# Residual and second norm of two batches moved into the next attention stage, with y turned to tokens ahead by VectorE, in a kernel of attention and triangle attention

## The chip, the cores and the metric

The kernel runs on one core of a Trainium2 chip. The time is device microseconds of one execution. Before the change it is 3651.67, the median of 3 runs (3650.98 to 3653.79). The engines are named as in the profile: PE is TensorE (PEld its weight loads), DVE is VectorE, ACT is ScalarE, POOL is GpSimd, SP is the engine whose queue issues most DMAs.

## The reference

Four images x of 64x64 pixels and 256 channels go through two layers. Layer 0 is self-attention over the 4096 pixels; layer 1 is triangle attention on the 64x64 grid with 8 heads, followed by an MLP. Only these lines of layer 1 matter for the change (x_in is the output of layer 0, called y in the kernel):

```
attn_out = out.reshape(B, N, N, E) @ Wo
h = x_in + attn_out
h = _layer_norm(h, ln_agg_g, ln_agg_b)
mlp = relu(h @ W1 + b1) @ W2 + b2
h = mlp + h
return _layer_norm(h, ln_out_g, ln_out_b)
```

A norm takes mean and variance over the 256 channels of a pixel (a token), so it is easy where tokens lie in the partitions and channels along the free side. Layer 0 leaves y the other way round, with channels in the partitions.

## The kernel before, in words

The batches are worked one after the other. Each batch has an attention stage (layer0) and then a triangle stage. The tokens of a batch, that is the code quoted above, run one stage later: next_layer1 for batch b, with b from 1 to 3, carries the tokens of batch b - 1. Batch 3's tokens have no later stage; two of their 16 tiles start in the triangle stage of batch 3, and the rest run in alone, the closing stage.

**Attention stage.** There are 8 query blocks of 512 pixels, each with 8 steps; a step is counted by g from 0 to 63, and k = g mod 8 is its place in its block. In a step TensorE makes four score tiles for the next step (L544) and multiplies four tiles of exponentials e with the values (L571); ScalarE takes the exponentials (L556); VectorE adds e into esum (L578), which frees one of e's two buffers. After each step comes a part of the block before it, from the list parts: k = 0 sums esum over partitions on TensorE (L596), takes the reciprocal on VectorE (L600), scales the output (L602) and reduces the denominators to bounds (L610); k = 1 projects the output to y (L623, L624 adds bias and input); k = 2 to 7 project y to q, k and the two values (L638, L670). In layer 0 of batch 0 VectorE also turns the other batches' inputs with 32x32 block transposes (L348), eight each second step. In the attention stages of batches 2 and 3, every third step brings one tile of finished tokens back from memory (recall) and GpSimd applies the last gain and shift (finish, L1248 and L1249). VectorE works its queue in the order of the program: values(g), the parts, and then whatever is added at the end of the step.

**Passage.** After step 63 the last block's output, its projections, the first loads of the triangle stage (fetch_v2, fetch_qk) and the first token tile are interleaved by hand, on queues of SP and ScalarE.

**Triangle stage.** There are 32 steps of 8 products (L999), made of attention weights and values, of 128x2048 elements each. In an even step 3 of the 8 products go to GpSimd and 5 to VectorE, in an odd step 2 and 6; TensorE adds each product up (L1009). Two steps and one token tile make a period. The order of a period is written by hand in ORDER: a word is an action, and /1 or /2 says how many periods late it runs. R05 is product 5 of the even step, A05 its accumulation, R1x and A1x those of the odd step; T takes an accumulator to SBUF; t turns weights on TensorE, c copies GpSimd's share of them to SBUF, S and W make the softmax sums and weights; sp and e are the scores of a later pair of heads and their exponentials. They end four tiles ahead of the stage's end. The triangle stage of batch 0 has an order of its own and no tokens. VectorE has three product buffers, GpSimd two. The words for tokens are:

- h0, h1: heads, TensorE: the attention output times Wo (L1081), and onto it y, turned to tokens by TensorE with the identity (L1086)
- sa: statistics of the sum, VectorE (L1097, L1098); rr: rsqrt for both norms as ln and exp, ScalarE (L1124, L1126); pp: a Newton step for both norms, seven small operations on GpSimd (L1142 to L1153)
- fa: the first norm applied, ScalarE (L1158); ht: h turned to channels, TensorE (L1181); hT and hU: two copies of it with gain and shift, ScalarE (L1186), one for the MLP and one as residual
- m, r, z: the MLP, TensorE and ScalarE (L1214, L1223, L1234); z also turns the residual copy back and adds it in PSUM (L1240)
- so: sums of the result for the second norm, ScalarE (L1112, L1116); fo: that norm applied, ScalarE (L1158); fi: the result stored (put_off) for recall in the next attention stage, or, for batch 3's stage, finished at once

**Closing stage.** alone works one tile of batch 3's tokens per round: heads, statistics on VectorE, MLP, with the residual and the second norm on VectorE (L1205, L1206, L1106).

## Time and profile before

| | us |
|---|---|
| median of 3 runs | 3651.67 |
| the profiled execution: its time | 3654.27 |
| its span | 3652.5 |
| a period of the triangle stage of batch 1, steady | 27.76 |
| a round of the closing stage | 9.51 |
| a transpose at L1086, mean | 0.273 |
| a product on VectorE (L999), mean | 2.274 |
| a product on GpSimd (L999), mean | 4.576 |

The profile is of one execution. A group's mean is the length of one instruction, and neighbouring instructions of one engine overlap in these records; what an engine has to pay for an instruction is the distance from its start to the next one's start, when nothing waits. Busy time of a stretch is the union of the records in it. "Idle before" is what the engine waited ahead of the instruction and for whom. In the stretches, x with a number is a count of instructions.

### The profile page before, as it was taken

Reading aid. Unit: us, or ns where it says so; the run is one execution under the profiler, and the core shown is the slowest. Engines: PE = TensorE matmul, PEld = TensorE weight load, DVE = VectorE, ACT = ScalarE, POOL = GpSimd, SP = SyncE. Lnnn points to the kernel's source line nnn. Section 1 sums busy time; section 2 is a strip of 40 time slices with the busy share of each in tenths; the row PEclk is TensorE's granted clock in tenths of the full one; section 3 lists DMA queues with packets and bytes.
Section 4 is the critical chain, followed back from the end, with each engine's and each line's share of the span. In section 5 each row is a group of like instructions: output and inputs, shape, how many; then the busy total and the mean of one; then the engine's idle time right before and its main releaser. Section 6 shows DMA issues by size and latency. Waiting matters only on the chain.

```text
span 3652.5 us, 58549 instructions
## 1 busy us (share of the span) xinstructions
PE 3544.0 (97%) x22410; PEld 1909.6 (52%) x22410; DVE 2739.5 (75%) x2326; ACT 1934.8 (53%) x4209; POOL 1805.7 (49%) x918
## 2 busy tenths in 40 slices
PE   9999899988999999999999999999999999999998
PEld 6555444434555555554455555554455555555477
DVE  4777599996555479999565549999755556999976
ACT  3444455544444367666444457676544436777654
POOL 5000199994000068889311028889722106999910
PEclk9999999999999999999999999999999999999999
DMA  9544555465111343425422153333522225341221
GB/s 174 140 130 121 137 150 143 118 135 126 52 49 52 97 116 95 94 51 104 101 80 79 58 144 92 78 89 66 129 73 78 75 83 137 91 96 47 68 69 52
DMA packets 487987, 353.38 MB, mean 97 GB/s; under 512 B 302673, under 2 KB 433489, under 8 KB 478865
## 3 DMA queue, kind: packets, MB, share of 16 engines
q1 hardware_dynamic: 438656, 322.58, 33.1%
q0 software_dynamic: 36160, 19.94, 5.1%
q10 hardware_dynamic: 12880, 7.01, 0.7%
q8 instruction: 179, 2.93, 0.3%
q14 instruction: 112, 0.91, 0.1%
HBM read 197.34 MB, written 152.04 MB: 96 GB/s over the span
## 4 chain that ended last, share of the span: by engine, by line
PE 68%; POOL 5%; DVE 4%; issue 3%; ACT 2%; DMA 1%; SPq 0%; ACTq 0%; DVEq 0%; POOLq 0%
PE o L571 18%; PE acc L1009 15%; PE proj L638 6%; PE mp L1214 6%; PE zp L1234 5%; PE s L544 5%; POOL Rp L999 4%; DVE R L999 3%; PE sp L897 3%; PE hp L1081 3%; PE v1p L670 2%; PE y L623 1%; PE att L951 1%; PE htp L1181 1%; PE hp L1086 1%
## 5 line engine op out<-in xcount | busy, mean ns | idle before, releaser
L999 POOL TENSOR_TENSOR Rp<-attP,v 128x2048 f32<-128x2048 f32 x328 | 1491.1, 4576 | 463.3 <-ACT attP L959 367.8
L999 DVE TENSOR_TENSOR R<-att,v 128x2048 f32<-128x2048 f32 x696 | 1547.7, 2274 | 67.7 <-PE acc L1009 49.4
L571 PE MATMUL o<-e,v 128*128 128x512 f32 x2048 | 1043.6, 592 | 0.0
L578 DVE TENSOR_TENSOR esum<-esum,e 128x2048 f32<-128x2048 f32 x224 | 525.0, 2344 | 508.9 <-ACT e L556 505.6
L556 ACT ACTIVATE e<-s 128x1024 f32<-128x1024 f32 x512 | 523.4, 1024 | 581.3 <-PE s L544 484.6
L544 PE MATMUL s<-gT,fT 128*128 128x512 f32 x1024 | 785.6, 769 | 8.6 <-ACT e L556 5.1
L1009 PE MATMUL acc<-R,wsel 128*32 128x512 f32 x5568 | 705.7, 602 | 37.2 <-DVE R L999 29.4
L571 PEld LDWEIGHTS o<-e,v 128*128 128x128 f32 x2048 | 388.7, 190 | 275.9 <-issue 233.6
L1009 PE MATMUL acc<-Rp,wsel 128*32 128x512 f32 x2624 | 344.3, 596 | 11.1 <-POOL Rp L999 10.4
L1019 ACT COPY ao<-acc 128x1024 f32<-128x1024 f32 x256 | 254.4, 1021 | 189.6 <-PE acc L1009 153.1
L1009 PEld LDWEIGHTS acc<-R,wsel 128*32 128x32 f32 x5568 | 152.1, 109 | 384.5 <-issue 277.9
L544 PEld LDWEIGHTS s<-gT,fT 128*128 128x128 f32 x1024 | 194.2, 190 | 243.9 <-issue 231.0
L1142 POOL TENSOR_SCALAR nt<-mv 128x4 f32<-128x4 f32 (+1 forms) x51 | 9.8, 192 | 627.2 <-DVE mv L1098 623.1
L1248 POOL TENSOR_TENSOR z<-z,log_bc 128x512 f32<-128x512 f32 x48 | 71.8, 1496 | 452.2 <-DMA z<-raw 434.5
L934 ACT ACTIVATE es<-S,rd 128x64 f32<-128x64 f32 x1024 | 257.8, 336 | 16.6 <-DVE rd L926 13.8
L1214 PE MATMUL mp<-hT,w 128*128 128x256 f32 x1024 | 249.5, 389 | 0.7 <-ACT hT L1186 0.7
L1234 PE MATMUL zp<-w,hid 128*128 128x256 f32 x1024 | 245.0, 385 | 0.8 <-ACT hid L1223 0.8
L1214 PEld LDWEIGHTS mp<-hT,w 128*128 128x128 f32 x1024 | 186.8, 190 | 101.2 <-ACT attP L959 36.0
L1234 PEld LDWEIGHTS zp<-w,hid 128*128 128x128 f32 x1024 | 185.7, 190 | 62.3 <-issue 29.3
L600 DVE RECIPROCAL rec<-den 128x512 f32<-128x512 f32 x32 | 107.4, 3358 | 119.4 <-PE den L596 114.0
L1009 PEld LDWEIGHTS acc<-Rp,wsel 128*32 128x32 f32 x2624 | 81.5, 110 | 197.8 <-issue 139.0
L1223 ACT ACTIVATE hid<-mp,b_sb 128x256 f32<-128x256 f32 x256 | 105.2, 469 | 117.7 <-PE mp L1214 117.7
(180 smaller groups left out, 3665.7 us busy)
## 6 DMA issues: line engine op xcount, KB each, us to landing
v<-v2d SPq DMA_DIRECT2D x44, 512.0 KB
v1c<-v1d SPq DMA_DIRECT2D x128, 128.0 KB
aT<-ao SPq DMA_DIRECT2D x1024, 16.0 KB
A<-aT SPq DMA_DIRECT2D x256, 64.0 KB
out_dram<-z SPq DMA_DIRECT2D x63, 256.0 KB
y<-yT SPq DMA_DIRECT2D x56, 256.0 KB
q<-st SPq DMA_DIRECT2D x56, 256.0 KB
k<-st SPq DMA_DIRECT2D x52, 256.0 KB
```

The source lines that it names most:

```text
L544: nc.tensor.matmul(s_ps[r // 2][:, r % 2, :], fT[tt][:, ts(r * 4 + n, P)], gT[qb // 4][:, ts(qb % 4, QB)], start=True, stop=not safe,)
L556: nc.scalar.activation(e[g][:, 2 * j : 2 * j + 2, :], s_ps[j], AF.Exp)
L571: nc.tensor.matmul(o_ps[qb], F.v[tt][:, r * 4 + n, :], es[:, r, :], start=(k == 0 and r == 0), stop=(k == 7 and r == 3),)
L578: nc.vector.tensor_tensor(esum[qb], esum[qb], es, ALU.add)
L638: nc.tensor.matmul(ps, w[:, cc, rows], y(qb, cc), start=(cc == 0), stop=(cc == 1))
L897: nc.tensor.matmul(sp[ts(h, 64), lh, n, :], k[rows, u * 8 + n, :], q[rows, u * 8 + n, :], start=True, stop=True,)
L934: nc.scalar.mul(e[:, i, :], rows[:, i, :], rec[:, i : i + 1])
L999: eng.tensor_tensor(R, src.unsqueeze(1).to_broadcast([P, D, N]), v2[h], ALU.mult)
L1009: nc.tensor.matmul(acc[32 * c : 32 * c + 32, n % 2, :], w[:, n, c, 16 * h : 16 * h + 32], R[:, ts(c, 8), :].rearrange("p d j -> p (d j)"), ...
L1019: nc.scalar.copy(self.ao[step][:, ts(np, 2)].rearrange("p k d j -> p k (d j)"), self.acc[step][np])
L1214: nc.tensor.matmul(self.mp[:, fc % 2, :], w1_sb[:, cc, ts(fc, P)], self.hT[tt][:, cc, :], start=(cc == 0), stop=(cc == 1),)
L1234: nc.tensor.matmul(zp[:, n, :], self.hid[tt][:, fc, ts(n, P)], w2_sb[:, fc, :], start=(fc == 0), stop=(fc == 3 and tt not in self.hT2),)
```

## The change

For the tokens of batches 0 and 1, the residual and the whole second norm leave the triangle stage. There the normed h (carried_off) and the MLP's result (summed_off) are stored separately, and in the attention stage of batches 2 and 3 a chain of six actions per tile, spread over eight steps, does the rest: recall (load of both), settle (VectorE: gain and shift of h, add, statistics), rooted (ScalarE), polished (VectorE), scaled (ScalarE) and finish (GpSimd as before). The statistics of the first norm, in these two stages, go from VectorE to ScalarE.

For batches 0, 1 and 3, y is turned to tokens when it is made: after the fourth step of a block VectorE turns it in square blocks of 32 (turn_y), and four DMAs write it to memory as tokens, for the last block in the passage. TensorE no longer turns it in heads; VectorE adds it to the heads in PSUM (add_y). For batch 2, whose tokens run in batch 3's triangle stage, nothing of this changes.

The triangle stages of batches 1 and 2 get a new order; batch 3's keeps the old one under the name ORDER_LAST. The softmax bounds are kept for one batch at a time and reduced at the start of the next attention stage. The tile that holds y for a token tile has two buffers where it had one.

```diff
 ORDER = """
+    sa R11/2 A13/2 A10/2 A11/2 T01/2 R12/2 sp/1 r0/1 e0/1 e1/1 t0/1 m1/1 R14/2 A12/2 A17/2 fo A14/2 R00/1 V0/1
+    R16/2 T10/2 r1/1 A16/2 c0/1 S1/1 W1/1 rr/1 R07/1 R15/2 A00/1 A15/2 z1/1 R01/1 T11/2 z0/1 pp/1 t1/1 R03/1
+    A01/1 R02/1 so/1 fa A07/1 A03/1 c1/1 R06/1 A02/1 ht hT S0 hU T00/1 fi/1 R05/1 h1/-1 V1/1 h0/-1 m0 R04/1
+    R13/1 W0 sf/1 R10/1 A04/1 A06/1 A05/1 f0/1 R17/1 f1/1
+""".split()
+
+
+ORDER_LAST = """
...
-    dens = ctile([P, NB, 256 + 16], "dens")
+    dens = ctile([P, 256 + 16], "dens")
+    lims = ctile([P, 2, NB], "lims")
+    def limits(b):
+        for j, op in enumerate((ALU.min, ALU.max)):
+            nc.vector.tensor_reduce(lims[:, j, b : b + 1], dens, AX.X, op)
...
-            for cc, tag in enumerate(("A", "yc")):
-                t = work.tile([P, 512], F32, tag=tag, name="yb", bufs=1)
+            for cc, tag, bufs in ((0, "A", 1), (1, "yc", 2)):
...
+        def turn_y(qb, **where):
+            t = work.tile([P, 16, 2, 32], F32, name="yr", **where)
+            for cc in range(2):
+                rows = y(qb, cc).rearrange("p (k t) -> p k t", t=32)
+                for k in range(4):
+                    nc.vector.transpose(t[:, ts(k, 4), cc, :], rows[:, ts(k, 4), :])
+            for r in range(4):
+                nc.sync.dma_start(
+                    out=io["yt"][ts(qb, QB), ts(r, 64)].rearrange("(k t) c -> t k c", t=32),
+                    in_=t[ts(r, 32)].rearrange("t k h c -> t k (h c)"),
+                )
 
...
+        if turned_ahead(b):
+            parts[3].append(lambda qb: turn_y(qb, tag="hid", bufs=1))
...
-            if b > 1 and g % 3 == 0 and g < 3 * NP:
-                rest.recall(NP * (b - 2) + g // 3)
-            if b > 1 and g % 3 == 2 and g < 3 * NP:
-                rest.finish(NP * (b - 2) + g // 3)
+            if b > 1:
+                for do, late in ((rest.finish, 7), (rest.scaled, 6), (rest.polished, 5), (rest.rooted, 4), (rest.settle, 3), (rest.recall, 0)):
+                    if (g - late) % 3 == 0 and 0 <= g - late < 3 * NP:
+                        do(NP * (b - 2) + (g - late) // 3)
+            if g == 1 and b > 0 and not safe:
+                limits(b - 1)
...
         bounds(last)
+        if turned_ahead(b):
+            turn_y(last, tag="k8")
...
-            rest.carried(t0)
+            (rest.carried if b == NB - 1 else rest.carried_off)(t0)
...
+    def turned_ahead(b):
+        return b != NB - 2
...
-        def put_off(self, tt):
+            self.raw, self.both, self.settled = {}, {}, {}
+
+
+        def put_off(self, tt, part, src):
             b, t = divmod(tt, NP)
-            if t == 0:
-                self.raw[b] = dram.tile([NP, P, 2, C], F32, tag="raw", name="raw")
-            nc.sync.dma_start(out=self.raw[b][t], in_=self.z.pop(tt))
+            if b not in self.raw:
+                self.raw[b] = dram.tile([NP, P, 2, 2, C], F32, tag="raw", name="raw")
+            nc.sync.dma_start(out=self.raw[b][t][:, part], in_=src)
+
+        def carried_off(self, tt):
+            self.put_off(tt, 0, self.h.pop(tt))
+
+        def summed_off(self, tt):
+            self.put_off(tt, 1, self.z.pop(tt))
         def recall(self, tt):
             b, t = divmod(tt, NP)
-            self.z[tt] = work.tile([P, 2, C], F32, tag="s4", name="z")
-            nc.sync.dma_start(out=self.z[tt], in_=self.raw[b][t])
+            self.both[tt] = work.tile([P, 2, 2, C], F32, tag="R", name="hz", bufs=3)
+            nc.sync.dma_start(out=self.both[tt], in_=self.raw[b][t])
+
+        def settle(self, tt):
+            both = self.both.pop(tt)
+            h, z = both[:, 0], both[:, 1]
+            nc.vector.tensor_tensor(h, h, lag_bc.unsqueeze(1).to_broadcast([P, 2, C]), ALU.mult)
+            nc.vector.tensor_tensor(h, h, lb2_bc.unsqueeze(1).to_broadcast([P, 2, C]), ALU.add)
+            nc.vector.tensor_tensor(z, z, h, ALU.add)
+            self.z[tt] = z
+            self.stats(z, 2)
+            self.settled[tt] = self.mv
+            self.mv = None
+
+        def rooted(self, tt):
+            self.mv = self.settled.pop(tt)
+            self.roots(2, 4)
+            self.settled[tt], self.mv = (self.mv, self.rs), None
+
+        def polished(self, tt):
+            self.mv, self.rs = self.settled.pop(tt)
+            self.polish(2, 4, nc.vector)
+            self.settled[tt] = self.rn
+
+        def scaled(self, tt):
+            self.rn = self.settled.pop(tt)
+            self.affine(self.z[tt], self.z[tt], 2)
...
-            nc.sync.dma_start(out=yc, in_=io["y"][:, ts(t, 256)].rearrange("(c p) t -> p c t", p=P))
-            self.A[tt] = A, yc
+            src = io["yt"][ts(t, 256)] if turned_ahead(b) else io["y"][:, ts(t, 256)]
+            nc.sync.dma_start(out=yt, in_=src.rearrange("(n p) c -> p n c", p=P))
+            self.A[tt], self.yt[tt] = A, yt
...
             for cc in range(2):
                 nc.tensor.matmul(
                     hp[:, n, :], A[:, cc, ts(n, 2), :].rearrange("p i j -> p (i j)"), wo1_sb[:, cc, :],
-                    start=(cc == 0), stop=False,
-                )
-            for cc in range(2):
-                nc.tensor.matmul(
-                    hp[:, n, ts(cc, P)], yc[:, cc, ts(n, P)], ident, start=False, stop=(cc == 1),
-                    is_transpose=True,
-                )
+                    start=(cc == 0), stop=(cc == 1 and turned_ahead(tt // NP)),
+                )
+            if not turned_ahead(tt // NP):
+                for cc in range(2):
+                    nc.tensor.matmul(
+                        hp[:, n, ts(cc, P)], self.yt[tt][:, cc, ts(n, P)], ident, start=False, stop=(cc == 1),
+                        is_transpose=True,
+                    )
+
+        def add_y(self, tt):
+            hp, yt = self.hps[tt], self.yt.pop(tt)
+            if not turned_ahead(tt // NP):
+                return
+            for n in range(2):
+                own = hp[:, n, :].rearrange("p (h r c) -> p h r c", h=2, r=4)
+                nc.vector.tensor_tensor(own, own, yt[:, n, :].rearrange("p (r h c) -> p h r c", h=2, r=4), ALU.add)
...
         def stats_a(self, tt):
+            self.add_y(tt)
...
             elif word == "sa" and first:
                 moments(q - 1)
-                rest.stats(rest.hps[t0 + q], 0)
+                rest.add_y(tt)
+                if own:
+                    rest.stats(rest.hps[tt], 0)
+                else:
+                    junk = work.tile([P, 2, C], F32, tag="sx", name="junk", bufs=1)
+                    rest.sums_of(rest.hps[tt], junk, rest.mv, 0)
             elif word == "so" and second:
+                z = rest.z[tt] = work.tile([P, 2, C], F32, tag="s4", name="z")
+                if own:
+                    moments(q)
+                    rest.sums_of(rest.zp[tt], z, rest.mv, 2)
+                else:
+                    nc.scalar.copy(z, rest.zp.pop(tt))
+            elif word == "rr" and second and (own or q + 1 < n1):
                 moments(q)
-                z = rest.z[t0 + q] = work.tile([P, 2, C], F32, tag="s4", name="z")
-                rest.sums_of(rest.zp[t0 + q], z, rest.mv, 2)
-            elif word == "rr" and second:
-                moments(q)
-                rest.roots(0 if q + 1 < n1 else 2, 4)
+                rest.roots(0 if q + 1 < n1 else 2, 4 if own else 2)
                 rs[q] = rest.rs
-            elif word == "pp" and second:
+            elif word == "pp" and second and (own or q + 1 < n1):
                 moments(q)
                 rest.rs = rs.pop(q)
-                rest.polish(0 if q + 1 < n1 else 2, 4, nc.gpsimd, back=back_t)
+                if own:
+                    rest.polish(0 if q + 1 < n1 else 2, 4, nc.gpsimd, back=back_t)
+                else:
+                    rest.polish(0, 2, nc.gpsimd, back=back_t[:, 2:4])
                 rn[q] = rest.rn
             elif word == "fa" and first:
                 rest.rn = rn[q - 1]
                 rest.affine_a(tt)
-            elif word == "fo" and second:
+            elif word == "fo" and second and own:
                 rest.rn = rn[q]
                 rest.affine_o(tt)
...
             elif word == "hU" and first:
-                rest.carried(tt)
+                (rest.carried if own else rest.carried_off)(tt)
...
-                (rest.finish if own else rest.put_off)(tt)
+                (rest.finish if own else rest.summed_off)(tt)
...
-            for word, late in words_of(ORDER):
+            for word, late in words_of(ORDER_LAST if own else ORDER):
                 i = period - late
-                if i == 0 and word in ("A05", "A04"):
+                if own and i == 0 and word in ("A05", "A04"):
```

More of the change, by code (lines that the diff above doesn't have):

```diff
@@ L445, in load @@
             self.y = []
-            for cc, tag in enumerate(("A", "yc")):
-                t = work.tile([P, 512], F32, tag=tag, name="yb", bufs=1)
+            for cc, tag, bufs in ((0, "A", 1), (1, "yc", 2)):
+                t = work.tile([P, 512], F32, tag=tag, name="yb", bufs=bufs)
                 nc.sync.dma_start(out=t, in_=self.io["y"][ts(cc, P), ts(q, 512)])
@@ L499, in layer0 @@
         io["v1"] = dram.tile([T, C], F32, tag="v1", name="v1d")
+        io["yt"] = dram.tile([T, C], F32, tag="yt", name="yt")
         L = Layer1(b, io, safe)
@@ L609, in bounds @@
                     c0 = 256 + 2 * qb + j
-                    nc.vector.tensor_reduce(dens[:, b, c0 : c0 + 1], t, AX.X, op)
+                    nc.vector.tensor_reduce(dens[:, c0 : c0 + 1], t, AX.X, op)
         def y(qb, cc):
@@ L922, in sums @@
             else:
-                den = dens[:, self.b, ts(step, IG)]
+                den = dens[:, ts(step, IG)]
             nc.vector.tensor_reduce(den, rows, AX.X, ALU.add)
@@ L1038, in __init__ @@
             self.ios = []
-            self.A, self.htp = {}, {}
+            self.A, self.yt, self.htp = {}, {}, {}
             self.h, self.hT, self.hT2, self.hid, self.z, self.zp, self.hps = {}, {}, {}, {}, {}, {}, {}
             self.mv = self.rs = None
-            self.raw = {}
-        def put_off(self, tt):
+            self.raw, self.both, self.settled = {}, {}, {}
+        def put_off(self, tt, part, src):
             b, t = divmod(tt, NP)
-            if t == 0:
-                self.raw[b] = dram.tile([NP, P, 2, C], F32, tag="raw", name="raw")
-            nc.sync.dma_start(out=self.raw[b][t], in_=self.z.pop(tt))
+            if b not in self.raw:
[5 more added lines that the diff above has]
+            self.put_off(tt, 1, self.z.pop(tt))
         def recall(self, tt):
             b, t = divmod(tt, NP)
-            self.z[tt] = work.tile([P, 2, C], F32, tag="s4", name="z")
-            nc.sync.dma_start(out=self.z[tt], in_=self.raw[b][t])
+            self.both[tt] = work.tile([P, 2, 2, C], F32, tag="R", name="hz", bufs=3)
[21 more added lines that the diff above has]
+            self.affine(self.z[tt], self.z[tt], 2)
         def load(self, tt, far=False):
@@ L1064, in load @@
                 both = big.tile([P, 2, 2, 256], F32, tag=tag, name="A", bufs=4 if tag == "v2" else 2)
-                A, yc = both[:, 0].rearrange("p c (i j) -> p c i j", j=N), both[:, 1]
+                A, yt = both[:, 0].rearrange("p c (i j) -> p c i j", j=N), both[:, 1]
             else:
                 A = work.tile([P, 2, 4, N], F32, tag="A", name="A", bufs=1)
-                yc = work.tile([P, 2, 256], F32, tag="yc", name="yc", bufs=1)
+                yt = work.tile([P, 2, 256], F32, tag="yc", name="yt", bufs=2)
             for c in range(2):
@@ L1078, in heads @@
             hp = self.hps[tt]
-            A, yc = self.A[tt]
+            A = self.A[tt]
             for cc in range(2):
@@ L1584, in attention_then_triangle_kernel @@
     lim = small.tile([P, 2], F32, tag="lim", name="lim", bufs=1)
-    flat = dens.rearrange("p b n -> p (b n)")
-    nc.vector.tensor_reduce(lim[:, 0:1], flat, AX.X, ALU.min)
-    nc.vector.tensor_reduce(lim[:, 1:2], flat, AX.X, ALU.max)
+    limits(NB - 1)
+    nc.vector.tensor_reduce(lim[:, 0:1], lims[:, 0], AX.X, ALU.min)
+    nc.vector.tensor_reduce(lim[:, 1:2], lims[:, 1], AX.X, ALU.max)
     nc.vector.tensor_scalar(lim[:, 0:1], lim[:, 0:1], 1e-25, None, ALU.is_ge)
```

## The prediction

> **What bounds the kernel now.** First the page's busy table:
>
> ```profile
> PE 3544.0 (97%) x22410; PEld 1909.6 (52%) x22410; DVE 2739.5 (75%) x2326; ACT 1934.8 (53%) x4209; POOL 1805.7 (49%) x918
> ```
>
> An average hides stages, so I asked for stretches of one period each in the stages the change touches. Columns: stretch, length, then busy us and count of PE, PEld, DVE, ACT, POOL, then clock, DMA share, GB/s.
>
> ```profile
> 1452.73:1480.50 27.77, 27.77 (x257) 14.98 (x260) 26.88 (x20) 19.63 (x55) 24.11 (x13) 1.00 0.19 49
> ...
> 1692.00:1720.00 28.00, 25.77 (x188) 11.13 (x180) 27.79 (x21) 17.97 (x53) 27.40 (x17) 1.00 0.73 147
> ...
> 3538.08:3547.59 9.51, 9.51 (x50) 8.38 (x49) 6.69 (x22) 5.26 (x14) 0.00 (x0) 1.00 0.31 84
> ```
>
> The first is the steady triangle stage of batch 1 (tokens of batch 0): TensorE has no gap in 27.76 us and VectorE 0.88 us of slack. The second is the end of that stage, where the score matmuls have run out: VectorE is full, GpSimd nearly, TensorE has room. The third is the closing stage of batch 3's tokens: TensorE full, VectorE 70%. The chain of waits agrees: PE 68% of the span, POOL 5%, DVE 4%. So TensorE time removed counts one for one in the first and third stretch, and hardly in the second.
>
> What TensorE does for one token tile, in the timeline (start, length):
>
> ```profile
> 1458.44 1.03 PE L1081 MATMUL hp<-wo,A 128*128 128x256 f32 x4
> 1459.31 0.38 PE L1086 MATMUL hp<-ident,yc 128*128 128x128 f32 x2
> 1459.53 1.03 PE L1081 MATMUL hp<-wo,A 128*128 128x256 f32 x4
> 1460.39 0.38 PE L1086 MATMUL hp<-ident,yc 128*128 128x128 f32 x2
> 1460.61 0.60 PE L1181 MATMUL htp<-ident,h 128*128 128x128 f32 x4
> ...
> 1477.73 0.38 PE L1240 MATMUL zp<-ident,hT 128*128 128x128 f32 x2
> 1477.95 1.89 PE L1234 MATMUL zp<-w,hid 128*128 128x256 f32 x8
> ```
>
> Lengths overlap; starts tell the pitch. Two transposes hold the engine 0.22 us (1459.31 to 1459.53, 1477.73 to 1477.95). A tile has four at L1086 and four at L1240: 8 x 0.109 = 0.87 us of 27.76.
>
> The groups, for VectorE (mean ns before the second bar):
>
> ```profile
> L1097 DVE BATCH_NORM_STATS2 st<-hp 128x6 f32<-128x256 f32 x128 | 52.8, 412 | 17.6 <-PE hp L1086 17.6
> ...
> L1304 DVE TENSOR_TENSOR z<-zp,z 128x256 f32<-128x256 f32 x2 | 0.8, 405 | 0.0
> ...
> L1205 DVE TENSOR_TENSOR z<-h,lag_bc 128x512 f32<-128x512 f32 x15 | 10.3, 685 | 0.0
> ```
>
> Last the attention stage, which receives work. Around a query block's end, VectorE:
>
> ```profile
> 2816.53 0.68 DVE L610 TENSOR_REDUCE dens<-den 128x1 f32<-128x512 f32 x1
> 2817.13 0.68 DVE L610 TENSOR_REDUCE dens<-esum 128x1 f32<-128x512 f32 x1
> 2817.72 2.28 DVE L578 TENSOR_TENSOR esum<-esum,e 128x2048 f32<-128x2048 f32 x1
> 2819.92 1.40 DVE L624 SCALAR_TENSOR_TENSOR yT<-y,bo_sb,yT 128x512 f32<-128x512 f32 x2
> ```
>
> and TensorE in the same stretch:
>
> ```profile
> 2822.84 1.88 PE L638 MATMUL proj<-yT,wq 128*128 128x512 f32 x4
> ```
>
> TensorE needs yT at 2822.84 and has it at 2821.3: 1.5 us of slack here, the least that I found in this stage, where TensorE is also gapless and VectorE about half busy (229.66 of 428 us).
>
> **What the Trainium skill says.** "TensorE: Matmul & The Clock Gate", Part 4 (PE-mode transpose), gives about 275 ns for a 128x128 transpose in a kernel; L1086 and L1240 have 273, but the pitch above, 109 ns, is what the queue pays. "VectorE: DVE Perf Modes", in its section on the TRN2 errata, prices an fp32 tensor_tensor at (N+151)/0.96 ns: 424 for N = 256; L1304, also PSUM with SBUF, took 405. "SBUF — State Buffer", Who interferes with whom: a VectorE operation with two SBUF inputs contends with a GpSimd one that reads SBUF. The trace agrees: L1249 in GpSimd took 1.27 us free and 3.20 beside VectorE. "DMA: Bandwidth & Descriptors", Specifications, puts line rate at 512 B and more; the new writes of y have 256 B. No run shows their price yet.
>
> **The change, part by part.**
>
> 1. *Transposes of y (L1086)* go for batches 0, 1 and 3 (192), *of the residual (L1240)* for batches 0 and 1 (128). In the stages of batches 1 and 2 the TensorE period becomes 27.76 - 0.87 = 26.89. In the closing stage it is 9.51 - 0.43 = 9.08.
>
> 2. *VectorE in these two stages.* Statistics of the heads move to ScalarE: bn_stats and bn_aggr, twice, held 1.16 us (1477.80 to 1478.96). Added: two adds of y. Bounds each: 0.28 (256 elements at L999's 2274/2048 ns) to 0.55 (L1304 with a dearer PSUM write); I take 0.40. VectorE: 26.87 - 1.16 + 0.80 = 26.5, still under 26.89.
>
> 3. *ScalarE* loses the second transposed copy (0.93), the affine of L1158 (1.0) and swaps sums of z for sums of the heads; it gains a 0.58 copy. 19.6 becomes about 18.3: no bound.
>
> 4. *The new order.* Laying its words on these durations with TensorE unbroken, I looked for waits. VectorE must lead by 1.4 us (R15 ends before A15), and may lead by up to 2.0 (R12 needs A13's buffer): possible. GpSimd's chain c0, R07, pp, R06, R05 ends at about 25.7, and A05 comes at 26.0: 0.3 us spare. So I take 26.9. The old period held for about 12 of 16 tiles; the last 4 ran at 27.3 (zp at 1694.84, then 1722.17), VectorE-bound, and get VectorE's 0.4. A stage saves 12 x 0.87 + 4 x 0.4 = 12.0; two save 24.0. Start and drain of the new order: between 2 lost and 2 won a stage, taken as 0.
>
> 5. *Closing stage.* 14 tiles x 0.43 = 6.0 saved. Adding y puts 0.8 on the path heads, statistics, ln, hT. It is covered: ln can wait for it because hT (1.0 long, done near 3546.2) is needed at 3547.28; TensorE itself comes 0.43 earlier, leaving some 0.3. Without that cover, up to 0.4 a tile goes back, 5.6.
>
> 6. *Attention stages of batches 2 and 3* get 16 settles each: three 128x512 operations in dependence (0.71 each) and statistics (1.04), 3.2 us on VectorE; four small operations for the polish, 0.8; two short and two 128x256 ScalarE operations, 1.5 in all. A settle comes every third step of 6.35 us, so its place walks through the block. At most places the queue behind it (esum, then the exp that needs e's buffer, then TensorE) has 3 us or more. At step 24 and 48 it lies between L610 and the esum at 2817.72: esum starts at 2821.0, the first L624 ends at 2823.95, and the projection waits 1.1 us. Four such: 4.5 lost. Bounds: 0, and 3 a place if GpSimd's finish blocks VectorE for 2 more: 12.
>
> 7. *Turning y ahead* (batches 0, 1, 3): 8 stream transposes a block; L348's 8 take 2.0 us on VectorE, at step 3, after which VectorE idles 3.4 us (2825.9 to 2829.31; in batch 0 3.5 us, one step later). Hidden. Their DMAs: 4 issues a block, some 2 us on SP; 2048 packets of 256 B. Queue 1 spends 33.1% x 16 x 3652.5 / 438656 = 44 ns a packet, so 5.6 us over 16 engines in a block of 50.8: share 0.60 to 0.71 in batch 0. Hidden. The last block's come in the passage to the triangle stage, ahead of the fetch of v2's last rows on SP, with the DMA share near 1.0 until 1284. The fetch issues at 1283.38 anyway; data slip up to 6 us, products start at 1300. I take 1 us in batch 0 (whose DMAs are busy until 450), 0.5 in batches 1 and 3: 2.0. Bounds 0 to 8.
>
> 8. *Stores and recall.* One more 256 KB store a tile in stages at DMA share 0.2 to 0.6, h's buffer free long before the next affine 27 us later; recall doubles to 512 KB, three steps (19 us) ahead. Nothing. The split of the final bounds: TensorE's cnt waits for zp, not for them. Nothing.
>
> Sum: -24.0 - 6.0 + 4.5 + 2.0 = -23.5. The profiled execution took 3654.27 (span 3652.5), so 3630.8 in its terms; the runs' median is 3651.67, which gives 3628.2.
>
> **Rivals.**
>
> - *Order short of TensorE's bound.* A wait of half the saving a period (GpSimd's 0.3 spare used up, or dearer adds). For: VectorE is left 0.4 slack, GpSimd's chain is long. Against: VectorE had only 0.88 before, and TensorE ran gapless. Stages save 2 x (12 x 0.4) = 10, sum -9.5: 3642.
> - *Small writes collide.* 256-byte writes cost several times 44 ns and delay loads in batch 0 and the passages: the upper bounds of 7, 6 more: 3634.
> - *All covers hold* (settles at 24 and 48 free, start-up shorter by 2 a stage): 3651.7 - 24 - 6 - 4 + 2 = 3620.
> - *Slower: the settle stalls TensorE everywhere.* If behind each of the 32 settles TensorE waited as at step 24, and GpSimd's finish blocked VectorE for 0.5 more, 32 x 1.6 = 51 would stand against 4.5: 3675. It decides from 28/32 = 0.9 us a settle on. Against: waits of VectorE for ScalarE of 3.0 to 5.5 us in most steps of this stage.
>
> **How the numbers follow.** My sum 0.58; order short 0.18; writes 0.08; covers 0.08; slower 0.08. 0.2% is 7.3 us, about what a measurement of this kernel can tell. Below 3644.4: all of sum, writes and covers, and 0.10 of order short: 0.84; within: 0.08; slower 0.08. Range 3619 to 3643, from the covers to order short.
>
> **What would show it.** Right: a period of 26.9 with TensorE gapless and VectorE near 26.5; 9.1 in the closing stage; 320 fewer transposes; hp adds near 0.4; projections at L638 late by about 1 us twice in each of the last two attention stages, and nowhere else. Wrong: TensorE gaps ahead of A05 or A15, adds over 0.6, a longer block of 50.8 us, loads that arrive late after the passages.

## The result: no change, and the profile after

The changed kernel takes 3653.25 us (median of 12 runs, 3646.26 to 3657.15) and the kernel before, on the same chips, 3652.99 (12 runs, 3648.44 to 3655.90): a ratio of 1.000, 95% interval 0.9991 to 1.0009. I had forecast 3628.2. The profiled execution took 3653.03, its span is 3651.2. First the busy line of the page after, then its chain of waits:

```profile
PE 3506.9 (96%) x22090; PEld 1875.5 (51%) x22090; DVE 2892.4 (79%) x2854; ACT 1932.0 (53%) x4221; POOL 1783.2 (49%) x904
...
PE 62%; POOL 17%; DVE 10%; issue 6%; ACT 2%; DMA 2%; SPq 0%; ACTq 0%; POOLq 0%; DVEq 0%
```

TensorE lost its 320 transposes and is 37 us less busy, yet the span is only 1.3 shorter: the chain now runs through GpSimd for 17% where it was 5%, through VectorE for 10% where it was 4%. The three stretches of the prediction, in the kernel after:

```profile
1432.33:1459.12 26.79, 26.71 (x252) 14.12 (x248) 26.54 (x18) 18.11 (x51) 24.12 (x13) 1.00 0.33 82
1692.00:1720.00 28.00, 23.57 (x172) 10.70 (x172) 26.13 (x17) 14.79 (x42) 27.09 (x17) 1.00 0.76 157
3541.00:3550.20 9.20, 9.20 (x46) 7.93 (x45) 7.47 (x25) 5.29 (x14) 0.00 (x0) 1.00 0.31 86
```

The steady period is 26.79 (forecast 26.9), VectorE 26.54 (26.5), ScalarE 18.1 (18.3), the closing round 9.20 (9.08). TensorE's work for one token tile, in the timeline after:

```profile
1435.40 0.66 PE L1262 MATMUL htp<-ident,h 128*128 128x128 f32 x4
1435.89 1.89 PE L1152 MATMUL hp<-wo,A 128*128 128x256 f32 x8
...
1454.53 3.72 PE L1315 MATMUL zp<-w,hid 128*128 128x256 f32 x16
```

The eight products of the heads and the sixteen of the MLP run on, with no transposes between them. So the steady work came out as forecast, and the time went elsewhere. To see where, I took the same marks in both traces: the last projection of an attention stage, the first, the 45th and the last accumulator that ScalarE takes in a triangle stage (L1054), and the end of TensorE's last instruction.

| stretch | before | after | change | forecast |
|---|---|---|---|---|
| batch 0, and attention of batch 1 | 1271.98 | 1274.28 | +2.3 | +1.0 |
| batch 1: start of the triangle stage | 45.55 | 53.93 | +8.4 | +0.5 |
| to the 45th accumulator | 307.78 | 296.33 | -11.4 | -10.4 |
| to the last | 119.19 | 121.15 | +2.0 | -1.6 |
| batch 2: attention | 399.71 | 403.11 | +3.4 | +2.25 |
| start of the triangle stage | 45.57 | 44.53 | -1.0 | 0 |
| to the 45th | 307.78 | 296.34 | -11.4 | -10.4 |
| to the last | 119.28 | 121.29 | +2.0 | -1.6 |
| batch 3: attention | 399.65 | 403.06 | +3.4 | +2.25 |
| triangle stage | 475.59 | 481.73 | +6.1 | +0.5 |
| closing | 147.15 | 143.80 | -3.4 | -6.0 |
| sum | | | +0.3 | -23.5 |

What follows TensorE's last instruction, 13.2 before and 11.7 after, is not in the sum; it was 11.3 to 12.9 in all other runs, so it is no effect of the change. The table compares one profile of each kernel, and the starts scatter: batch 2's, 44.53 here, was 45.93 to 47.79 in five runs that leave its passage as the change has it (e1, e2, e4, e6, e7), and batch 3's, 51.93 here, was 50.53 to 51.50 in e3, e4 and e7.

Four things took the gain: the starts of the two stages in whose passage y is turned (14.5, where batch 3's 6.1 is of its whole stage), the ends of two stages (4.0 lost where 3.2 were to be won), the attention stages (6.8 where 4.5 were forecast), and a smaller gain in closing.

**The start of batch 1's stage.** SP's queue in the passage; first the kernel before, then after:

```profile
1283.38 2.29 SPq L880 DMA_DIRECT2D v<-v2d  x4
1285.76 7.09 SPq L1071 DMA_DIRECT2D A<-aT  x4
```

```profile
1287.44 6.81 SPq L653 DMA_DIRECT2D yt<-yr  x4
1294.30 5.85 SPq L915 DMA_DIRECT2D v<-v2d  x4
1300.24 6.84 SPq L1141 DMA_DIRECT2D A<-aT  x4
```

The four writes of turned y hold SP for 6.81 us. The A of the second token tile stands behind them and is issued by 1307.08 instead of 1292.85. Most of this time is waiting, not issuing: before the fourth write SP waits 3.7, before the fourth load of v's rows 4.4 and before the fourth load of A 4.8, each time for a store that ScalarE has issued (v1d<-stage, q<-stage and v2d<-st). In this trace the DMAs of SP and of ScalarE signal their end on the same eight semaphores (100 to 107), and SP starts each of these three 0.02 after the store before it on the same semaphore has landed. The chain of waits after goes through the last of them:

```profile
1303.52 0.59 ACT st L679
...
1304.14 2.56 DMA v2d<-st
...
1306.72 1.95 DMA A<-aT
...
1308.80 2.91 PE hp L1152 x6
```

So the last load of A could not go before 1306.70, however early SP came to it: four more DMAs in the common sequence of SP and ScalarE put it behind a later store. TensorE after:

```profile
1303.32 0.59 PE L1152 MATMUL hp<-wo,A 128*128 128x256 f32 x2
1308.80 2.90 PE L1152 MATMUL hp<-wo,A 128*128 128x256 f32 x6 [4.89 <-DMA A<-aT]
1315.03 1.93 PE L1044 MATMUL acc<-R,wsel 128*32 128x512 f32 x8 [3.33 <-DVE R L1034]
```

and VectorE after:

```profile
1311.80 0.90 DVE L1169 TENSOR_TENSOR hp<-hp,yt 128x256 f32<-128x256 f32 x2 [14.17 <-PE hp L1152]
1312.61 2.28 DVE L1034 TENSOR_TENSOR R<-att,v 128x2048 f32<-128x2048 f32 x1
```

TensorE waits 4.89 for A; and since the new order puts sa, now with the adds of y, ahead of the first product, VectorE stands idle for 14.17 before the adds, while its first product (1300.03 before) could have run. TensorE then waits 3.33 for that product. The stretches of 4 us there show a third loss, in the granted clock, the third number from the right:

```profile
1304.00:1308.00 4.00, 0.00 (x0) 0.00 (x0) 0.00 (x0) 0.11 (x1) 3.25 (x1) 0.93 0.29 75
1308.00:1312.00 4.00, 2.90 (x6) 1.85 (x6) 0.20 (x1) 0.00 (x0) 0.00 (x0) 0.50 0.44 138
1312.00:1316.00 4.00, 0.97 (x8) 0.23 (x8) 3.93 (x6) 2.12 (x9) 0.19 (x1) 0.50 0.55 148
1316.00:1320.00 4.00, 4.00 (x15) 2.52 (x8) 4.00 (x2) 2.18 (x10) 1.31 (x7) 0.50 1.04 240
```

After the idle time TensorE has half its clock for 13.6 us, until past 1320 (the next 4 us have 0.87). The Trainium skill, "TensorE: Matmul & The Clock Gate", section "Why this matters for your kernels", advises against gaps of TensorE of more than about 3 us, because it falls back to half rate; this passage agrees, with 0.50 after a wait of 4.89. But 3 us is no sharp limit here: in e2 (below) the clock stayed at 1.00 through a wait of 3.37, and in e11 it fell to 0.50 for 3.4 us after one of 2.27.

**The steady period.** The chain of waits through one period of the kernel after:

```profile
1425.81 4.56 POOL Rp L1034
...
1432.33 9.08 POOL Rp L1034 x2
...
1441.44 3.64 PE acc L1044 x32
1445.09 1.91 PE sp L932 x64
1447.00 0.59 PE att L986 x4
1447.59 1.73 PE mp L1295 x8
1449.32 1.04 PE acc L1044 x8
...
1451.42 0.84 ACT hid L1304 x2
1452.26 0.22 ACT attP L994
...
1452.60 4.56 POOL Rp L1034
```

It is a loop of 26.79: three products and a polish on GpSimd, accumulations and scores on TensorE, a copy for GpSimd on ScalarE. In the kernel before, the same view shows TensorE alone. TensorE is no longer the bound: from start to start its instructions need 26.51, and the other 0.28 is waiting ahead of accumulations. VectorE is close behind: its starts add to 26.56, with one wait of 0.23 a period for an accumulation. No run takes the GpSimd loop out, so this bound is read from the trace; without the loop VectorE's 26.56 would be the next.

**The attention stage** at step 24 of batch 2, VectorE after (three settle operations, its statistics, then the esum and the output that had been next):

```profile
1896.74 0.68 DVE L1104 TENSOR_TENSOR hz<-hz,lag_bc 128x512 f32<-128x512 f32 x1
...
1900.00 2.26 DVE L593 TENSOR_TENSOR esum<-esum,e 128x2048 f32<-128x2048 f32 x1
1902.17 1.40 DVE L639 SCALAR_TENSOR_TENSOR yT<-y,bo_sb,yT 128x512 f32<-128x512 f32 x2
```

and TensorE:

```profile
1902.97 1.98 PE L667 MATMUL proj<-yT,wq 128*128 128x512 f32 x4 [0.95 <-DVE yT L639]
```

This wait comes four times in the trace, at steps 24 and 48 of batches 2 and 3, as forecast, and at no other projection from yT.

### The profile page after: what moved, and what is told of

The parts are those of the page before. It is cut to its first block, busy times and chain, and to the rows that moved or that the text cites. A ratio compares the mean times of both kernels' runs of the same rounds, so it can differ in the third digit from the quotient of the medians.

```text
span 3651.2 us, 58663 instructions
## 1 busy us (share of the span) xinstructions
PE 3506.9 (96%) x22090; PEld 1875.5 (51%) x22090; DVE 2892.4 (79%) x2854; ACT 1932.0 (53%) x4221; POOL 1783.2 (49%) x904
## 4 chain that ended last, share of the span: by engine, by line
PE 62%; POOL 17%; DVE 10%; issue 6%; ACT 2%; DMA 2%; SPq 0%; ACTq 0%; POOLq 0%; DVEq 0%
PE o L586 22%; POOL Rp L1034 15%; PE acc L1044 10%; PE proj L667 8%; PE s L559 6%; DVE R L1034 4%; PE sp L932 3%; PE mp L1295 3%; PE v1p L699 2%; PE zp L1315 2%; PE y L638 1%; PE hp L1152 1%; DVE rec L615 1%; PE att L986 1%; DVE st L1177 1%
## 5 line engine op out<-in xcount | busy, mean ns | idle before, releaser
L586 PE MATMUL o<-e,v 128*128 128x512 f32 x2048 | 1043.4, 592 | 0.0
L593 DVE TENSOR_TENSOR esum<-esum,e 128x2048 f32<-128x2048 f32 x224 | 517.5, 2310 | 366.3 <-ACT e L571 363.6
L1044 PE MATMUL acc<-R,wsel 128*32 128x512 f32 x5568 | 697.9, 600 | 34.7 <-DVE R L1034 28.9
L586 PEld LDWEIGHTS o<-e,v 128*128 128x128 f32 x2048 | 388.3, 190 | 277.1 <-issue 233.9
L1054 ACT COPY ao<-acc 128x1024 f32<-128x1024 f32 x256 | 257.4, 1017 | 188.1 <-PE acc L1044 144.1
L1329 POOL TENSOR_TENSOR hz<-hz,log_bc 128x512 f32<-128x512 f32 x32 | 48.4, 1513 | 541.8 <-ACT hz L1239 473.1
L1223 POOL TENSOR_SCALAR nt<-mv 128x2 f32<-128x2 f32 (+1 forms) x49 | 9.4, 192 | 575.7 <-DVE mv L1178 561.8
L1315 PEld LDWEIGHTS zp<-w,hid 128*128 128x128 f32 x1024 | 189.4, 191 | 68.2 <-ACT es L969 23.5
L942 ACT ACTIVATE S<-sp 128x512 f32<-128x512 f32 x128 | 128.9, 1110 | 96.3 <-PE sp L932 95.4
```

The lines of the kernel that those rows point to most:

```text
L586: nc.tensor.matmul(o_ps[qb], F.v[tt][:, r * 4 + n, :], es[:, r, :], start=(k == 0 and r == 0), stop=(k == 7 and r == 3),)
L593: nc.vector.tensor_tensor(esum[qb], esum[qb], es, ALU.add)
L1044: nc.tensor.matmul(acc[32 * c : 32 * c + 32, n % 2, :], w[:, n, c, 16 * h : 16 * h + 32], R[:, ts(c, 8), :].rearrange("p d j -> p (d j)"), ...
L1054: nc.scalar.copy(self.ao[step][:, ts(np, 2)].rearrange("p k d j -> p k (d j)"), self.acc[step][np])
L1315: nc.tensor.matmul(zp[:, n, :], self.hid[tt][:, fc, ts(n, P)], w2_sb[:, fc, :], start=(fc == 0), stop=(fc == 3 and tt not in self.hT2),)
```

## The experiments

Theory: the steady gain is real, and is given back where the four writes hold SP in the passages (stages of batches 1 and 3), in the settles, and in the ends of the stages. Main rivals: the new order alone makes the starts late; the small packets fill the DMA engines, not the queue. Below, "start" is the first row of a stage in the table above, "period" is the steady one. Ratios are to the kernel before, with 95% intervals.

### The passages

**e1_gpsimd_queue**

```diff
-            turn_y(last, tag="k8")
+            turn_y(last, nc.gpsimd, tag="k8")
```

> The changed kernel, with the four writes of the last block's turned y in each passage issued by GpSimd instead of SP. Theory: in the passages the four writes hold the SP queue for 6.8 us (1287.44 to 1294.25), and v's last rows and the A of the next token tile, which stand behind them, issue 6 to 7 us late; the first product starts 9.4 us late after batch 1 and 6.4 after batch 3. Freed of the queue, A(next) issues near 1288 again and the stages of batches 1 and 3 get back 6 each and the passage of batch 0 some 2: 14 less than the changed kernel, 3639. Rival 1 (the new order, which puts sa ahead of the first product, makes the start late): batch 1's start stays late by 9, batch 3's goes, 5 less: 3648. Rival 2 (the small packets fill the DMA engines, not the queue): the data come as late as before, no change, 3653.

Measured: 3641.15, ratio 0.9966 (0.9954 to 0.9979). Start of batch 1's stage 46.10, of batch 3's 45.55 (before 45.55 and 45.54). SP in this kernel:

```profile
1288.63 7.73 SPq L915 DMA_DIRECT2D v<-v2d  x4
1296.46 4.86 SPq L1141 DMA_DIRECT2D A<-aT  x4
```

GpSimd issued the four in 2.61. The same bytes go out in the same passage, some 3 us earlier, and the two starts are back, so it is the place in SP's queue, not the packets' load on the DMA engines, and not VectorE's eight block transposes, which are still there. GpSimd's DMAs signal on other semaphores in this trace, and the last load of A waits for an earlier store of ScalarE (q<-stage, landed at 1300.94). No run separates the time that the writes hold SP from the later store that A then waits for; in the trace of the kernel after it is the store that comes last. "DMA: Bandwidth & Descriptors", section "Issuing engines are not separate DMA queues", says that another issuing engine saves only the time of issue, usually little; here the other engine was worth 12 us of the kernel, since with it went waits.

**e2_late_writes**

```diff
+        if turned_ahead(b):
+            write_y(last, yr)
         if not late:
             values1(1)
```

> The changed kernel, with the block transposes of the last block left where they are, and its four writes issued on SP behind the next tile's A and y. Theory (queue): v's rows and A go first, 12 to 15 less than the changed kernel, 3638 to 3641; what is held up behind the writes now is only k, q and v of the next pair, and these have time. Rival 1 (order): 5 less, 3648. Rival 2 (packets fill the DMA engines): v and A now come ahead of the packets too, so the gain is the same as for the queue, 12 to 15; only the run with the GpSimd queue tells these two apart.

Measured: 3640.09, ratio 0.9966 (0.9952 to 0.9979); starts 44.53 and 45.57. As the theory has it.

**e3_sa_later**

```diff
+                elif word == "sa" and period == 1 and not own:
+                    pass
                 else:
+                    if word == "rr" and period == 1 and not own:
+                        of_piece("sa", period)
```

> The changed kernel, with sa of the first period of the two new-order stages moved behind the first product, just ahead of rr; nothing of the writes is changed. Theory (queue): TensorE still waits for A(next) at 1308.8, but VectorE has up to three products ready by then; of the 9.4 late in the stage of batch 1 about 3 to 4 come back, in that of batch 2 (no turned y in its passage) about 0 to 1, batch 3 none: 3649. Rival 1 (order alone): the stage of batch 1 gets all 9 back: 3644. Rival 2: as the theory.

Measured: 3644.49, ratio 0.9980 (0.9972 to 0.9988); start of batch 1's stage 47.71 (6.2 back), of batch 2's 41.19 (3.3 back). More than the theory gave it, and in total rival 1's number, but not by its mechanism: TensorE still waits 4.80 for A, and then finds products ready. So the place of sa takes part in the late start, and the two losses add to more than 8.4, because the new order without them starts some 4 earlier than the old (e5, e11).

**e8_old_order_plus_writes**: the kernel before with only the last block's turn_y in the passages.

```diff
         bounds(last)
+        if b != NB - 2:
+            turn_y(last, tag="k8")
```

> The kernel before, with nothing of the change but the last block's turning of y and its four writes in the passages of batches 0, 1 and 3; nobody reads what they write. Theory (the writes hold SP's queue): the stages of batches 1 and 3 start 6 to 7 late each and batch 0's 1 to 2 late: 13 to 15 more than the kernel before, 3666. Rival (the delay of batch 1 is the new order's): batch 1's start is as before, 7 more: 3659.

Measured: 3664.88, ratio 1.0037 (1.0023 to 1.0051). Starts 50.76 and 50.90: 5.2 and 5.4 lost, with the old order. SP waits 4.8 for v2d<-st in batch 1's passage here too. The writes suffice, without the new order.

### The settles

**e4_settle_shift**

```diff
-                    if (g - late) % 3 == 0 and 0 <= g - late < 3 * NP:
-                        do(NP * (b - 2) + (g - late) // 3)
+                    for t in range(NP):
+                        if g == 3 * t + late + (late > 0 and t in (7, 15)):
+                            do(NP * (b - 2) + t)
```

> The changed kernel, with settle and what follows it one step later for the two tiles whose settle falls on the first step of a query block (steps 24 and 48), so that the block's output on VectorE goes ahead of it. Theory: each of the four stalls of 1.2 us of the projection goes, 4.8 less: 3648. Rival (the loss of 2.4 and 2.6 in these stages is spread over all settles, or over recall and finish): 1 or less, 3652 to 3653.

Measured: 3649.84, ratio 0.9995 (0.9987 to 1.0004), too near to 1 to tell by itself. The trace tells: the two attention stages are 400.51 and 400.52 long, 2.6 and 2.5 shorter, and no projection from yT waits. Of the 3.4 lost in each, 0.8 to 0.9 stays. In batch 2 it lies at steps 8 and 9 alone (0.36 and 0.45 by the starts of L586): the steps before them are short (4.35, later ones 6.07), a settle at step 6 makes the end of their block late on VectorE, and at step 8 TensorE waits 0.27 for its output oT.

### The triangle stages

**e5_no_turned_y**

```diff
     def turned_ahead(b):
-        return b != NB - 2
+        return False
```

> The changed kernel without its y part: no batch turns y ahead, TensorE turns it in heads as before and nothing is added by VectorE; the second norm in the next attention stage and the new order stay. Theory: the passages lose nothing to writes, so batch 1's stage starts about as before and batch 3's exactly; the period rises from 26.8 to 27.2 (four transposes of 0.109 are back), and the closing stage is as before (3.4 back). Against the kernel before: two stages 4.5 to 5 shorter each plus 1 at the start, attention stages 3.4 longer each, sum -4: 3648. Rival (the new order's sa makes the starts late): batch 1's stage still starts 8 late, 3656. Rival (the new order gains by itself, not by fewer transposes): the period stays at 26.8 and the sum is -12: 3640.

Measured: 3633.16, ratio 0.9948 (0.9935 to 0.9962): 20 better than with turned y, and better than every expectation; the nearest was the rival that the new order gains by itself. Its steady period:

```profile
1439.36:1466.30 26.94, 26.94 (x252) 14.56 (x248) 25.87 (x16) 18.02 (x52) 24.13 (x13) 1.00 0.22 60
```

TensorE turns y again and is gapless, in 26.95, not in the 27.2 that I expected. The starts of both stages are 41.55, 4.0 earlier than in the kernel before; here sa has no adds of y that could hold VectorE. My theory had missed something in TensorE itself, so the next run takes the order out.

**e12_no_y_old_order**

```diff
-            for word, late in words_of(ORDER_LAST if own else ORDER):
+            for word, late in words_of(ORDER_LAST):
```

> As e5_no_turned_y (no y part; residual and second norm in the next attention stage), but with the old order in the stages of batches 1 and 2 too. Theory: of the 0.81 a period that e5 gained, 0.44 are the four transposes that went with the residual and 0.37 are the new order's (the MLP's first product 0.20, the accumulations 0.14, the turning of h 0.04, in which TensorE's weight loads are less in the way). With the old order the period is 27.32 and the stage starts as before: 2 x (14 x 0.44) gained, 6.8 given back in the attention stages: 5 less than the kernel before, 3648. Rival (the order is worth nothing by itself): as e5, 3633.

Measured: 3644.33, ratio 0.9980 (0.9972 to 0.9988); starts 44.63 and 44.61; period:

```profile
1445.14:1472.46 27.32, 27.32 (x252) 14.56 (x248) 25.86 (x16) 18.45 (x52) 24.07 (x13) 1.00 0.22 59
```

27.76 - 0.44 = 27.32: the four transposes cost what their pitch says. The other 0.37 is the new order's. Distances from start to start, summed over one period: the MLP's first product 3.85 in the old order and 3.65 in the new, the accumulations 14.28 and 14.15, the turning of h 0.53 and 0.49. The difference stands where the kind of matmul changes. In the old order the MLP follows accumulations; the load of its weights then begins with its first matmul (0.483 long), and the next follows after 0.320. In the new order it follows the heads; the load begins 0.107 ahead, the first matmul takes 0.382 and the next follows after 0.219.

**e7_spread_on_sp**

```diff
     def spread_g(F, r, d, half):
-        nc.gpsimd.dma_start(
+        nc.sync.dma_start(
```

(and spread_f alike)

> The changed kernel with the 12 DMAs that spread the next batch's factors at the end of each triangle stage of batches 0 to 2 issued by SP instead of GpSimd, on which they take 0.67 each. Theory: in the last four tiles of the stages of batches 1 and 2 GpSimd is the bound (five products of 4.55, a polish of 2.0 and four issues of 0.67 are 27.4, the period there); freed, these periods come down to some 26.6: 2 to 3 a stage, 4 to 5 in all: 3648. Rival 1 (VectorE bounds the tail, as I forecast): no change, 3653. Rival 2: SP waits with them for the factors and holds stores and loads behind them: 0 to 10 slower.

Measured: 3656.28, ratio 1.0007 (1.0000 to 1.0014). The ends of the two stages, to the last accumulator, did gain 2.3 and 3.2: from one MLP output to the next, batch 1's last periods are 26.55, 26.55 and 25.75, where the kernel after has 27.06, 27.37 and 27.64. There GpSimd after shows no gap:

```profile
1672.49 1.36 POOL L274 DMA_DIRECT2D gT<-ahgf  x2
1673.85 13.66 POOL L1034 TENSOR_TENSOR Rp<-attP,v 128x2048 f32<-128x2048 f32 x3
1687.44 1.32 POOL L274 DMA_DIRECT2D gT<-ahgf  x2
```

But the helper also serves the front of batch 0, which I had overlooked: batch 0 ended 4.3 later than in the kernel after, and the attention stages of batches 2 and 3 were 0.9 and 0.6 longer. The end of batch 0 scatters, though: with the same batch 0, e3, e4 and e6 end it 1.9 to 3.3 later than the kernel after. So GpSimd bounded the tail; that the move makes batch 0 late is not shown, and e13 leaves batch 0 out of it.

### Which batches, and the mends together

**e6_turned_y_01** (return b < 2)

> The changed kernel with y turned ahead for batches 0 and 1 only; batch 3's y is turned by TensorE as before. Theory: the 6.4 late start of batch 3's triangle stage goes, the 3.4 saved in the closing stage go too: 3 less than the changed kernel, 3650. Rival (packets in the 8 blocks of batch 3's attention stage cost too): more, up to 6: 3647.

Measured: 3652.66, ratio 1.0000 (0.9991 to 1.0008). Batch 3's start is 45.58 and closing 147.1, both as before the change; the 3 can't be seen in the whole, whose interval is 3 to either side; in this profile batch 0 was 3 longer than in the kernel after's.

**e9_no_y_settle** (e5 and e4 together)

> Without the y part (as e5_no_turned_y), and with the settles of steps 24 and 48 one step later (as e4_settle_shift). Theory: the two edits touch different stages, so their gains add: -19.8 and -5.0 against the kernel before: 3628. Rival (what the run without y gained was chance or a shifted state of the queues, not the period): less than 12 against before, 3641.

Measured: 3631.32, ratio 0.9944 (0.9931 to 0.9958). The attention stages of batches 2 and 3 are each 0.9 longer than in the kernel before, where e5's are 3.2 and 3.3 longer. The sum of the medians' gains is 21 for the theory's 25, within the interval.

**e11_y_mended** (e2, e3 and e4 together)

> The changed kernel with y turned ahead for batches 0, 1 and 3 as it is, and three mends: the writes in the passages behind the next tile's loads, sa of the first period behind the first product, the settles of steps 24 and 48 one step later. Theory: -12.9 for the writes, -3.3 a stage for sa in both stages, -5.0 for the settles, all against the changed kernel: 3653 - 12.9 - 6.6 - 5.0 = 3628, that is as good as the version without turned y, no better, since VectorE's adds give back 0.28 of the 0.44 that a period gains, and the blocks' writes cost batch 0 some 4. Rival (turned y is worth its full 0.44 a period once the passages are mended): 5 to 8 better than the version without it, 3621.

Measured: 3632.00, ratio 0.9944 (0.9931 to 0.9958), as good as e9 and no better. The expectation named the wrong reason: by the chain shown above it is the GpSimd loop, not VectorE's adds, that keeps the period at 26.79. And the late writes have a price of their own here: in batch 1's stage the first period (four accumulators) is 32.48 where e2 has 28.42. The loads of the next heads' q and k stand behind the writes (the last k is issued by 1318.52), the chain of waits runs through them, and TensorE is idle for 2.27 ahead of these heads' scores. So what the new place of sa gains at the start of this stage (41.27 where e2 has 44.54) goes again in its first period, and e11 shows turned y with this price on it. No run has all three mends without it.

**e13_y3_mended**: y turned ahead for batch 3 only with late writes, e4's settles, and from batch 1's stage on the factor DMAs on SP. sa stays where the new order has it: in these two stages it has no adds.

> The best version that the runs so far point to: y turned ahead for batch 3 only, with its last writes behind the next loads (the closing stage gains 3.4); residual and second norm in the next attention stage, settles of steps 24 and 48 one step later (5.0); in the stages of batches 1 and 2 the factor DMAs on SP instead of GpSimd (3 a stage). Against the kernel before: -19.8 - 5.0 - 3.4 - 6 = -34: 3619. Rival (in the version without y the tail has another bound, TensorE turning y, and the factor DMAs' move brings nothing): 3625.

Measured: 3622.57, ratio 0.9928 (0.9914 to 0.9942), the best of all: 30 less than the kernel before by the medians, 26 by the ratio. The tail, 1625.06 to 1651.64, has VectorE 25.87 and GpSimd 24.08 of 26.58; closing is 3.5 shorter. The attention stages of batches 2 and 3 are 2.1 and 2.0 longer than before, 1.3 and 1.1 more than in e9.

### Batch 0

In the profiles up to here batch 0's triangle stage ended 2.1 to 6.5 late in the kernels that turn its y in all blocks, and 0.3 to 4.1 early in those that don't turn it; with the last block's alone (e8) it ended 1.5 late.

**e14_old_blocks_of_0** (turn_y in parts[3] of the kernel before, batch 0)

> The kernel before, with nothing of the change but the turning of y and its four writes in batch 0's attention blocks 0 to 6 (not the last block, not in the passage); nobody reads what they write. Theory (the blocks are not hidden in batch 0, whose DMA engines are 0.6 busy with the next batches' work): batch 0's attention stage ends 2 to 3 later than before and the whole is 2 to 3 longer: 3655. Rival (as forecast: hidden): no change at the last projection of batch 0 and in the whole, 3652.5.

Measured: 3653.99, ratio 1.0005 (0.9997 to 1.0014).

**e15_old_passage_of_0** (turn_y(last) in its passage, batch 0)

> The kernel before, with nothing of the change but the turning of the last block's y and its four writes in the passage of batch 0; nobody reads what they write. Theory: the first accumulator of batch 0's triangle stage is taken 5 to 6 later, and the stage, which waits for memory anyway, makes 4 of it good: 1 to 2 at the end, 3654. Rival (the passage is the whole of batch 0's loss): 4 to 6, 3658.

Measured: 3654.61, ratio 1.0006 (0.9997 to 1.0014).

**e16_y_1_3_mended** (e11 with b in (1, NB - 1))

> As e11_y_mended (writes behind the loads, sa behind the first product, settles one step later), with y turned ahead for batches 1 and 3 only. Theory: batch 0's loss of 4 to 6 goes; batch 1's stage has TensorE turn y again, 16 x 0.16 = 2 to 3 more: 2 to 3 better than e11, 3629. Rival (batch 0's times scatter from run to run, and turning y there costs nothing): 2 to 3 worse than e11, 3634.5.

Measured: 3629.62, ratio 0.9940 (0.9927 to 0.9954), near the theory's 3629, and within e11's interval. Neither part alone costs more than about 5 us (0.14%), and each may cost nothing. The ends of batch 0 in e14 and e15 are +1.0 and -0.8. How the loss divides stays open.

## Why the prediction was wrong, step by step

1. *Transposes.* Right: 0.109 each, shown by e12's 27.32.
2. *VectorE.* Right: two adds hold it 0.80 (428 ns each in the records); it was busy 26.54 against 26.5.
3. *ScalarE.* Right.
4. *The new order.* The period was right by luck: two errors cancel. I priced TensorE at the old order's durations; the new one needs 0.37 less, so its own sum is 26.95 - 0.44 = 26.51. And the 0.3 that GpSimd's chain had to spare was no spare against this: it holds the period at 26.79. Of the 0.44 for y's transposes only 26.95 - 26.79 = 0.16 a period is left. In the last four tiles I named VectorE as the bound; it was GpSimd, whose factor DMAs (0.67 each, four a period) I had not counted: 2.0 lost a stage where I had 1.6 won. The start was taken as 0. Where no y was turned it was -1.0 in the table's profile and +0.4 to +2.2 in five others; with sa out of the way it is -4.3 (e3, e11), so the place of sa cost 3 to 7 in batch 2's stage, and up to 6.2 in batch 1's (e3), which this step had put at nothing.
5. *Closing.* Mis-sized: 3.4, not 6.0. My cover looked at one wait (hT) and not at VectorE as a loop. The first rounds do take 9.07; from the seventh on they take 9.20. The chain of waits there:

```profile
3545.45 0.45 DVE hp L1169
3545.92 0.44 DVE hp L1169
3546.39 0.44 DVE st L1177
...
3554.65 0.45 DVE hp L1169
```

Adds, statistics, ln, rs and residue follow each other on VectorE and ScalarE, 9.20 a round; TensorE, alone in this chain before, is not in it. These rounds cost about 0.8 of the forecast. Another 1.4 goes in the last but one, which takes 9.18 where it took 7.73: TensorE waits 1.55 for hid there, 0.22 before.
6. *Settles.* Right in place and number; 1.2 a stall for 1.1. Another 0.8 to 0.9 a stage is no stall of the projection (e4): a settle can be late for the block's end too, a place that I took as covered.
7. *Turning y.* This is the step that failed. It put a block's four issues at "some 2 us on SP" and said that "the fetch issues at 1283.38 anyway". In the passage the four took 6.81, and fetch and A stood behind them. What I had left out is what SP waits for between issues, the landing of ScalarE's stores: 3.7 of the 6.81, and then 4.8 ahead of the last load of A, for which TensorE waited 4.89. I had 0.5 each for batches 1 and 3; it was 8.4 and 6.1, more than the upper bound of 8 for all three, and in batch 1's stage the place of sa (step 4) has its part in the 8.4. I had seen that SP is moved past, but priced its issues from a free stretch, though A's four issues in the same passage showed 7.09 before, 5.2 of it a wait for such a store (v1d<-stage).
8. *Stores.* Nothing seen that speaks against it.

No rival foresaw it: "small writes collide" had the place but not the mechanism (e1), "order short" had GpSimd's spare used up, but reckoned with TensorE's old sum.

## What to carry to other kernels

Price a DMA's issue by what the same queue shows in the same stretch, not by its cost when the queue is free. List what stands behind it, and look in the trace for what each issue waits for: it may be a DMA of another engine. Where the next loads start a stage, let them go first. When TensorE is relieved, follow the loop through the other engines over one whole period: here GpSimd's loop left 0.16 of 0.44. Test the parts of a change singly: the second norm with the new order was worth 20 us (e5), and turning y ahead, with its writes and adds where this change has them, undid it. With both moved it neither cost nor gained (e11 against e9), and for batch 3 alone it gained in closing (e13).

## What the runs showed of the hardware

- Four issues on SP, 128 KB each, took 6.81 us in the passage, 3.7 of it a wait for a store of ScalarE to land; four on GpSimd took 2.61 there (e1).
- SP and ScalarE share eight semaphores for the end of their DMAs in these traces, and a DMA of SP starts only when the one before it on its semaphore has landed, also where that is ScalarE's: 4.8 lost ahead of A in the kernel after, 5.2 in the kernel before.
- After a wait of 4.89, TensorE had a granted clock of 0.50 for 13.6 us, in which it was partly idle again; after waits of 4.80 (e3) and 2.27 (e11) for 3.4 us, after one of 3.37 (e2) not at all. In the kernel before, its longest wait there is 0.55 and the clock stays 1.00.
- The order of TensorE's own instructions was worth 0.37 in 27.32, with the same instructions (e12 against e5): TensorE has no idle time in either period. A change from accumulations to the MLP costs 0.10 more than one from the heads.
